# Sparse attention in a graph network: one-hot matrices in a narrow and a wide size, the summing matmuls six tiles behind them, one exponential for two rows, the edge weights applied one row later

## The chip, the cores and the metric

The kernel runs on one core of one Trainium2 chip. The metric is the device time of one execution in microseconds (us). The kernel before took 4278.34 us, the median of three runs (4271.37 to 4294.40).

## What is computed

The reference is a stack of four blocks over 6250 nodes with 256 features each: a graph convolution, a mixture of experts whose routing is a graph attention, a second graph convolution, and a second mixture of experts. The change is in the second block only. Cut to what matters (`_L0_ffn_ref`), it is:

```python
h = (x_flat @ W_gat).reshape(M, HEADS, NUM_EXPERTS)          # 4 heads, 4 experts
src = concat([edge_index[0], loops]); dst = concat([edge_index[1], loops])
e = leaky_relu(a_src[src] + a_dst[dst], 0.2)
ee = exp(e - e_max[dst])
denom = segment_sum(ee, dst)
msg = h[src] * (ee / (denom[dst] + 1e-16))[:, :, None]
agg = segment_sum(msg, dst) + b_gat                          # 131072 edges
scores = layernorm(agg).reshape(M, HEADS, NUM_EXPERTS).mean(1)
topk_s, topk_i = top_k(scores, 2); w = softmax(topk_s)
out = sum over experts of  gate * (gelu(x @ W1[e] + b1[e]) @ W2[e] + b2[e])
```

So each edge needs an attention weight, an exponential of a sum of two node values, and the weighted values of the edges are added up by destination node.

## The kernel before, in words

The program is built by a layer that tracks which instruction reads and writes which buffer, adds the semaphore waits, and gives out buffers from pools of fixed depth (`bufs`). It orders the instructions of each engine by itself: an instruction keeps about the place in which the Python code issues it, unless its buffer is not yet free in the layer's own reckoning; then later instructions go ahead of it. After that each engine runs its instructions strictly in that order.

By the time of the attention stage the edges have been sorted by destination. They stand in tiles of 128 edges, one edge to a partition; `tiles2` lists 84 rows (`NA`) with 8 tiles each (`G`), fewer in the last eleven, 612 tiles in all. The destinations of one tile lie within n neighbouring blocks of 128 nodes, with n from 1 to 7 (`NM` is 7). In most rows the first and the last tile are wide (4 to 7 blocks) and the six between them have at most 3. From row 68 on nearly all tiles are wide, and the last rows have one tile each.

The sum by destination is a matmul. For a tile, VectorE writes a one-hot matrix `E` of 128 edges by n times 128 nodes in bf16 (`spread_out`, L1964): one where the edge's destination is the node. TensorE then multiplies it with the tile's values (`add_up`, L1986), one matmul for each block, and adds the tiles of a row up in the PSUM banks `po`; after the row's last tile VectorE adds `po` to `acc` (L1997). The values come in three bf16 parts, so that the sum is as exact as in fp32: they stand in `pays0` and `pays1`, which the rows use in turn.

One pass of the main loop has number k and works on five rows at once. `fetch(k)` starts the gathers of row k from `gat_dram` into `sg` (GpSimd's indirect DMAs, L1173). `score(k - 2)` multiplies the one-hot rows `rb` with the nodes' values on TensorE (`pa`, L1909). `weigh(k - 3)` picks from `pa` (L1926), sums (L1931), adds the gathered value (L1932), applies the leaky ReLU (L1933) and the exponential on ScalarE (L1934). `weight(k - 3, 0)`, at the end of the same pass, multiplies the gathered values with the exponentials (`pay`, L1946) and writes the first bf16 part (L1951); its steps 1 and 2 (L1953 to L1956) follow in the next pass. `spread_out` runs on row k - 4, two tiles in each of four places of the pass, and `add_up` runs `LAG` tiles behind it:

```python
EB, LAG = 6, 4
Es[g, j] = wk.tile([P, NM, P], BF16, name="E", bufs=EB)
g, j = divmod(there * G + q - LAG, G)        # the tile that add_up takes
```

The pools set how far the engines can run apart: six `E` buffers, all as wide as the widest tile, four `sg`, two `z`, two `pays`.

Between these steps a `slot` is called five times in a pass. It advances three queues of other work. `experts1` computes all experts of the block for all nodes: in each step four fp32 products `ph` (L1160) with Gelu on ScalarE (L1787), or four products `py` (L1160) and their bias on VectorE (`ys`, L1803), written to DRAM. `routing` holds `gates`, the normalisation and the choice of experts for windows whose sums are complete. `steps` holds `node_values`, which adds the chosen experts to `x_all` (L2185) and prepares the next block: a square root (L2196), transposes (L2215, L2226) and the table `hp_dram` (L2229); in the first passes it holds `edge_columns`, which reads the edges of the next block into `hp` and `ht` tiles. In the first 17 passes `count_last` also counts edges of one node (`q`, `b`, L2005 to L2017). The Exp, Gelu and Sqrt functions each need another table in ScalarE, and the program has an ACT_TABLE_LOAD wherever the function changes.

After the loop the queues are emptied, and the next block starts to gather from `hp_dram` (`hg`).

Of the kernel before, what the change touches and what calls it, by code (L numbers as in the profile page):

```python
# [9 lines left out]
F32 = mybir.dt.float32  # L10
# [7 lines left out]
P = 128  # L18
# [889 lines left out]
BF16 = mybir.dt.bfloat16  # L908
# [3 lines left out]
def kernel(ctx: ExitStack, tc: tile.TileContext, a: dict, out: bass.AP):  # L912
# [78 lines left out]
    with ExitStack() as fast:  # L991
# [845 lines left out]
        with (  # L1837
# [35 lines left out]
            pa_both = psa.tile([P, 2, G, 256 // G], F32, name="pa")  # L1873
            assert NM * H <= 256 // G
            HG = G // 2
            EB, LAG = 6, 4
            rows, near, got, pas, zs, pay, Es, pos = {}, {}, {}, {}, {}, {}, {}, {}

            def tiles_of(g, half):
# [7 lines left out]
                return rb  # L1887

            def fetch(g):
                got[g] = wk.tile([P, G, GW], F32, name="sg", bufs=4)  # L1890
                for j in range(len(tiles2[g])):
                    gather(got[g][:, j, :], gat_dram, src2[:, g * G + j : g * G + j + 1])

# [29 lines left out]
            def weigh(g):  # L1923
                m, n = len(tiles2[g]), union[g][2]
                za = wk.tile([P, G, NM, H], F32, name="za", bufs=1)[:, 0:m, 0:n, :]
                V.tensor_mul(  # L1926
                    za, pas.pop(g)[:, 0:m, 0 : n * H].rearrange("p g (b h) -> p g b h", h=H),
                    near.pop(g)[:, 0:m, 0:n].unsqueeze(3).to_broadcast([P, m, n, H]),
                )
                z = wk.tile([P, G, H], F32, name="z")[:, 0:m, :]  # L1930
                V.tensor_reduce(z, za.rearrange("p g b h -> p g h b"), axis=AX.X, op=OP.add)  # L1931
                V.tensor_add(z, z, got[g][:, 0:m, HV:])  # L1932
                V.scalar_tensor_tensor(z, z, 0.2, z, op0=OP.mult, op1=OP.max)  # L1933
                SC.activation(z, z, AF.Exp)  # L1934
                zs[g] = z

            for (u0, u1, _), some in zip(union, tiles2):
                assert {b for lo, n in some for b in range(lo, lo + n)} == set(range(u0, u1))
# [19 lines left out]
            def spread_out(g, j):  # L1958

                if j >= len(tiles2[g]):  # L1960
                    return
                n = tiles2[g][j][1]
                Es[g, j] = wk.tile([P, NM, P], BF16, name="E", bufs=EB)
                V.tensor_scalar(  # L1964
                    Es[g, j][:, 0:n, :].rearrange("p b k -> p (b k)"), nodes16[:, 0 : n * P],
                    bits.bitcast(F32)[:, g * G + j : g * G + j + 1], None, op0=OP.is_equal,
                )
# [272 lines left out]
            def edge_columns():  # L2240

                GP.iota(from_i, pattern=[[P, NC]], base=0, channel_multiplier=1)
                V.tensor_scalar(from_n, from_i, float(NS), None, op0=OP.mult)
                V.tensor_copy(from_i, from_n)
                V.tensor_scalar(from_i, from_i, 8, None, op0=OP.logical_shift_right)
                V.tensor_copy(from_n, from_i)
                V.tensor_scalar(from_n, from_n, -44.0, 0.0, op0=OP.add, op1=OP.max)
                V.tensor_scalar(from_n, from_n, float(NP - NW), None, op0=OP.min)
                for c in range(NC):
                    n = min(P, T1 - c * P)  # L2250
                    at = slice(c * P, c * P + n)
                    for name, none in (("src", 0), ("dst", 2**24), ("edge_weight", 0)):
                        ap = n6.tile([P, P], F32, name="hp")
                        raw = ap.bitcast(I32)
                        ap = ap if name == "edge_weight" else raw
                        full = min(c * P + n, C1) - c * P
                        if full < n:
                            V.memset(raw, none)
                            e = a[name][C1 * P : E1].rearrange("(o p) -> o p", o=1)
                            SY.dma_start(ap[full:n, 0 : E1 - C1 * P], e)  # L2260
                        rows_of = a[name][c * P * P : (c * P + full) * P]
                        SY.dma_start(ap[0:full, :], rows_of.rearrange("(t p) -> t p", p=P))
                        yield False
                        f = n6.tile([P, P], F32, name="ht")
                        if name == "dst":
                            V.tensor_scalar(
                                f[0:n, :], raw[0:n, :], from_n[0:n, c : c + 1], None,
                                op0=OP.subtract,
                            )
                        else:  # L2270
                            V.tensor_copy(f[0:n, :], ap[0:n, :])
                        yield False
                        pt = psy.tile([P, 2, D], F32, name="py")[:, 0, 0:n]
                        TE.transpose(pt, f[0:n, :], ident[0:n, 0:n])
                        if name == "src":
                            g = n6.tile([P, P], F32, name="ht")[:, 0:n]
                            V.tensor_scalar(g, pt, 0.0, float(N), op0=OP.is_lt, op1=OP.mult)
                            V.tensor_add(g, g, pt)
                            V.tensor_scalar(
                                src_of[:, at], g, 0.0, float(N - 1), op0=OP.max, op1=OP.min  # L2280
                            )
                        else:
                            SC.activation((dst_of if name == "dst" else ew)[:, at], pt, AF.Copy)
                        yield False

                hit = wk.tile([P, G, P], BF16, name="rb")
                hit = hit.rearrange("p g k -> p (g k)")[:, 0:T1]
                V.tensor_scalar(hit, dst_of, -0.5, None, op0=OP.is_gt)
                V.scalar_tensor_tensor(
                    hit, dst_of, NW - 0.5, hit, op0=OP.is_lt, op1=OP.mult  # L2290
                )
                V.tensor_reduce(good2[:, 5:6], hit, axis=AX.X, op=OP.add)
# [23 lines left out]
                    steps.append([node_values(ws), False])  # L2316

            def slot(n=1):
                if n and (k < NA or k == NA + 5 or slots[0] % 5 == 0):
                    advance(layers, n)  # L2320
                slots[0] += 1
                run(steps, False)
                load_outputs()
                start_steps()
# [5 lines left out]
            def complete(t1):  # L2330

                while ends and ends[0] <= t1:
                    waiting.append((passed[0], ends[0] - passed[0]))
                    passed[0] = ends.pop(0)
# [6 lines left out]
            ]  # L2341
            remaining = [min(u[0] for u in union[g:]) for g in range(NA)] + [T]
            counted = False
            for k in range(NA + 5):
                if k < NA:
                    fetch(k)
                if k == 1:
                    own_edges()
                now, here, there = k - 2, k - 3, k - 4

                def spread_and_sum(i):

                    for q in (2 * i, 2 * i + 1):
                        if there in range(NA):
                            spread_out(there, q)
                        g, j = divmod(there * G + q - LAG, G)
                        if g in range(NA):
                            add_up(g, j)

                if there in range(NA):  # L2360
                    weight(there, 1)
                spread_and_sum(0)
                slot()
                if now in range(NA):
                    score(now, 0)
                slot()
                if there in range(NA):
                    weight(there, 2)
                spread_and_sum(1)
                if here in range(NA):  # L2370
                    weigh(here)
                tables()
                run(routing, False)
                slot()
                spread_and_sum(2)
                slot()
                if now in range(NA):
                    score(now, 1)
                run(routing, False)
                slot(int(k < 62))  # L2380
                if here in range(NA):
                    weight(here, 0)
                spread_and_sum(3)
                for _ in range(4):
                    if last_columns:
                        count_last(*last_columns.pop(0))
                if not last_columns and not counted:
                    routing.append([last_edges(), False])
                    counted = True
                if counted and k - 5 in range(NA):  # L2390
                    complete(remaining[k - 4])
            V.tensor_reduce(good2[:, 0:1], acc[:, :, 3 * HV], axis=AX.X, op=OP.add)
            k = NA + 5
            while layers or steps or routing or waiting or done["begun"] < T:
                slot()
                tables()
# [400 lines left out]
```

## Time and profile before

| what | value |
| --- | --- |
| median of three runs | 4278.34 us |
| profiled execution | 4285.28 us |
| its span, first to last instruction | 4283.5 us |
| mean granted TensorE clock | 0.831 |
| attention stage in the span | about 1580 to 2920 us |
| TensorE, VectorE, ScalarE, GpSimd busy in the stage | 1020, 704, 576, 597 us of 1340 |
| granted clock in the stage | 0.87 |

The profile is of one execution, 6.9 us above the median. Busy time is the time in which an engine has at least one instruction at work. A row of a group of instructions gives the line, the engine, the operation, the tiles that are written and read, the form, the count, the busy time, the mean duration in ns, and the idle time of the engine just before them with what ended it. A row of the waits gives the engine and the instruction that waited, what ended the wait, the sum in us, how often, and the longest. "issue" means that the profile shows nothing that was waited for, and "remote" that a semaphore ended the wait and no instruction of the record is near enough to be its source.

### The profile page before, as it was taken

To read this page: it belongs to the slowest core of one execution; us is meant where nothing else is said; L and a number is where in the kernel's file an instruction comes from. 1 tells how busy PE (TensorE), PEld (TensorE's weight loads), DVE (VectorE), ACT (ScalarE), POOL (GpSimd) and SP (SyncE) were. 2 spreads that over 40 slices of the span, in tenths; PEclk is the share of its full clock that TensorE was granted. 3 is DMA by queue.
4 is the path that set the end of the run, shared out by engine and by line. 5 is a ranking of instruction groups with operands and counts; after the bars stand their busy time and mean duration, and the time that the engine had idled before them with its cause. 6 is when DMAs were issued, how large, how long until landed. Compare 5 with 4: busy or idle time off the path is not lost.

```text
span 4283.5 us, 59672 instructions
## 1 busy us (share of the span) xinstructions
PE 3272.3 (76%) x19189; PEld 2500.2 (58%) x19189; DVE 2166.2 (51%) x6247; ACT 1188.7 (28%) x2203; POOL 2257.1 (53%) x2720
## 2 busy tenths in 40 slices
PE   6798888888888785777887877785346777877787
PEld 4566666666666564566665666573244555555566
DVE  7576666666555444545463544575123333333344
ACT  4122222222222232334444343463011211211123
POOL 1655655566565544345454444422666666665651
PEclk9899999999999897888998988796567667677678
DMA  5677776777676642223333332343111111111110
GB/s 172 158 172 164 167 161 157 161 171 165 159 168 153 147 108 58 61 65 100 84 99 78 81 89 67 87 109 90 45 46 52 47 51 51 50 51 48 53 47 19
DMA packets 698942, 429.43 MB, mean 100 GB/s; under 512 B 530968, under 2 KB 639563, under 8 KB 698620
## 3 DMA queue, kind: packets, MB, share of 16 engines
q0 software_dynamic: 88512, 177.73, 17.3%
q1 hardware_dynamic: 366812, 188.25, 16.4%
q10 hardware_dynamic: 243296, 59.53, 7.0%
q8 instruction: 155, 2.54, 0.3%
q14 instruction: 167, 1.37, 0.1%
HBM read 382.75 MB, written 42.50 MB: 99 GB/s over the span
## 4 chain that ended last, share of the span: by engine, by line
PE 36%; another core or an unknown queue 14%; issue 6%; DVE 5%; ACT 3%; DMA 1%; POOL 1%; DVEq 0%; ACTq 0%; SPq 0%
PE ph L1160 13%; PE py L1160 11%; PE pe L2662 5%; PE pt L1160 2%; PE po L1986 2%; PE pa L1909 1%; DVE eq L2641 1%; POOL hg L1173 1%; DVE E L1964 1%; DVE x_all L2617 1%; ACT L1787 0%; ACT hh L1787 0%; PE pe L1609 0%; PE pt L1154 0%
## 5 line engine op out<-in xcount | busy, mean ns | idle before, releaser
L1173 POOL DMA_INDIRECT h<-y_dram,src x882 | 858.4, 973 | 669.0 <-issue 485.7
L1173 POOL DMA_INDIRECT hg<-hp_dram,src x831 | 784.9, 944 | 490.7 <-issue 225.0
L1173 POOL DMA_INDIRECT sg<-gat_dram,src x612 | 593.8, 970 | 723.1 <-DVE pay L1946 313.8
L1160 PE MATMUL ph<-w1b,et 128*128 128x256 f32 x3528 | 868.2, 398 | 32.8 <-issue 26.9
L1160 PEld LDWEIGHTS ph<-w1b,et 128*128 128x128 f32 x3528 | 680.3, 198 | 204.4 <-issue 114.3
L1160 PE MATMUL py<-w,hh 128*128 128x256 f32 x1568 | 454.0, 428 | 105.6 <-issue 54.5
L2662 PEld LDWEIGHTS pe<-eq,hg 128*128 128x128 f32 x2036 | 375.3, 261 | 189.8 <-issue 117.5
L2662 PE MATMUL pe<-eq,hg 128*128 128x96 f32 (+15 forms) x2036 | 386.4, 342 | 126.2 <-issue 67.2
L1586 DVE TENSOR_TENSOR h<-ph,h 128x1536 f32<-128x1536 f32 x147 | 258.2, 1757 | 421.1 <-remote 158.6
L1160 PE MATMUL ph<-b_all,w 128*128 128x256 f32 (+1 forms) x1600 | 458.9, 426 | 11.8 <-issue 11.5
L2641 DVE TENSOR_SCALAR eq<-px,dst,ew 128x96 f32<-128x96 f32 x831 | 261.1, 367 | 320.1 <-remote 131.4
L1587 ACT ACTIVATE h<-h 128x1536 f32<-128x1536 f32 x147 | 218.2, 1484 | 728.6 <-DMA ea<-in_edge_attr_dram 288.4
L1160 PEld LDWEIGHTS py<-w,hh 128*128 128x128 f32 x1568 | 308.1, 210 | 171.1 <-issue 70.2
L1160 PEld LDWEIGHTS ph<-b_all,w 128*128 128x128 f32 x1600 | 316.9, 214 | 55.5 <-issue 17.4
L1964 DVE TENSOR_SCALAR E<-nodes,bits 128x256 bf16<-128x256 bf16 (+5 forms) x612 | 187.6, 340 | 194.4 <-remote 73.3
L1609 PE MATMUL pe<-h,eq 128*32 128x257 f32 x3168 | 256.7, 416 | 36.3 <-issue 35.2
L1568 DVE STREAM_TRANSPOSE et<-ea 128x1536 f32<-128x1536 f32 x147 | 260.5, 1773 | 12.7 <-issue 9.3
L1787 ACT ACTIVATE hh<-ph,b 128x256 f32<-128x256 f32 (+1 forms) x400 | 166.5, 467 | 306.8 <-remote 166.5
L1160 PE MATMUL py<-ew,g 65*128 65x256 f32 x392 | 146.6, 503 | 57.5 <-DVE x_all L2617 42.1
L1609 PEld LDWEIGHTS pe<-h,eq 128*32 128x32 f32 x3168 | 104.7, 116 | 143.6 <-issue 91.1
L1986 PE MATMUL po<-pays,E 128*128 128x61 bf16 x2116 | 120.0, 199 | 48.1 <-issue 41.8
L1160 PE MATMUL ph<-b_all,ew 128*128 128x512 f32 (+2 forms) x256 | 115.4, 576 | 53.4 <-ACT g L2577 33.8
(355 smaller groups left out, 3971.7 us busy)
## 6 DMA issues: line engine op xcount, KB each, us to landing
ea<-in_edge_attr_dram ACTq DMA_DIRECT2D x588, 96.0 KB
ea<-in_edge_attr_dram SPq DMA_DIRECT2D x588, 96.0 KB
w<-in_L_ffn_W_dram SPq DMA_DIRECT2D x48, 512.0 KB
y<-ys SPq DMA_DIRECT2D x96, 256.0 KB
rb<-low_dram SPq DMA_DIRECT2D x84, 256.0 KB
h<-y_dram,src POOLq DMA_INDIRECT x882
hg<-hp_dram,src POOLq DMA_INDIRECT x831
gtab<-y SPq DMA_DIRECT2D x100, 128.0 KB
```

The costliest lines, as they stand in the source:

```text
L1160: TE.matmul(dst, lhs(c), rhs(c), start=c == 0, stop=c == n - 1)
L1173: GP.indirect_dma_start(out=dst, out_offset=None, in_=table[0:NP, :], in_offset=IndirectOffsetOnAxis(ap=idx, axis=0),)
L1568: V.transpose(et[q].rearrange("p c m k -> p m c k"), ahead.pop(q).rearrange("p i m (c k) -> p (i m) c k", c=2),)
L1586: V.tensor_add(h, ph.pop(q), h)
L1587: SC.activation(h, h, AF.Relu)
L1609: TE.matmul(sums[w][b * Q : (b + 1) * Q, :], eq[k][:, j, at], h[:, i * NT + j, 0:WS], start=g == 0 and j == NT - 1, stop=g == last_of[b] a ...
L1787: SC.activation(hidden[u][:, f, :n, :], ph[:, f - f0, :n, :], AF.Gelu, bias=b1[:, e, f : f + 1],)
L1909: TE.matmul(pas[g][:, j, 0 : n * H], rows[g][:, j, :], part[:, i, b0 : b0 + n, :].rearrange("p t h -> p (t h)"), start=i == 0, stop=i == 2,)
L1964: V.tensor_scalar(Es[g, j][:, 0:n, :].rearrange("p b k -> p (b k)"), nodes16[:, 0 : n * P], bits.bitcast(F32)[:, g * G + j : g * G + j + 1 ...
L1986: TE.matmul(pos[g][bank][:, to * HP : (to + 1) * HP], E[:, b - b0, :], pays[g % 2][:, j, :], start=bank not in begun, stop=bank not in lat ...
L2641: V.tensor_scalar(equals[k][:, j, :], lanes[:, 0:NW], dst_of[:, t : t + 1], ew[:, t : t + 1], op0=OP.is_equal, op1=OP.mult,)
L2662: TE.matmul(sums[b][:, lo - t0 * P : hi - t0 * P], hg[:, j, :], eq[:, j, lo - n0 : hi - n0], start=False, stop=after >= (t0 + n) * P,)
```

## The change

There are five edits. The one-hot matrices come from two pools: eight buffers of 3 blocks for tiles with n up to 3 (`E`), three buffers of 7 blocks for the others (`Ew`). `LAG` is 6 instead of 4. The exponential is taken at every odd row for that row and the row before, in one instruction where the two have as many tiles and in two instructions one after the other where not; for this `z` holds two rows. `weight` runs one row later (steps 0, 1 and 2 on rows k - 4, k - 5, k - 5), and `spread_out` and `add_up` with it, so that the loop has one pass more and `sg` five buffers. In `edge_columns`, `ht` has one buffer, and the tile for wrapped sources takes the name `hp`.

```diff
-            EB, LAG = 6, 4
+            NARROW, LAG = 3, 6
...
-                got[g] = wk.tile([P, G, GW], F32, name="sg", bufs=4)
+                got[g] = wk.tile([P, G, GW], F32, name="sg", bufs=5)
...
-                z = wk.tile([P, G, H], F32, name="z")[:, 0:m, :]
+                if g % 2 == 0:
+                    zs[g] = wk.tile([P, 2, G, H], F32, name="z")
+                both = zs[g - g % 2]
+                z = both[:, g % 2, 0:m, :]
...
-                SC.activation(z, z, AF.Exp)
-                zs[g] = z
+                if g % 2:
+                    for i in range(2):
+                        zs[g - 1 + i] = both[:, i, 0 : len(tiles2[g - 1 + i]), :]
+                    if len(tiles2[g - 1]) == m:
+                        SC.activation(both[:, :, 0:m, :], both[:, :, 0:m, :], AF.Exp)
+                    else:
+                        for i in range(2):
+                            SC.activation(zs[g - 1 + i], zs[g - 1 + i], AF.Exp)
...
-                Es[g, j] = wk.tile([P, NM, P], BF16, name="E", bufs=EB)
+                if n <= NARROW:
+                    Es[g, j] = wk.tile([P, NARROW, P], BF16, name="E", bufs=8)
+                else:
+                    Es[g, j] = wk.tile([P, NM, P], BF16, name="Ew", bufs=3)
...
-                        f = n6.tile([P, P], F32, name="ht")
+                        f = n6.tile([P, P], F32, name="ht", bufs=1)
...
-                            g = n6.tile([P, P], F32, name="ht")[:, 0:n]
+                            g = n6.tile([P, P], F32, name="hp")[:, 0:n]
...
-                if n and (k < NA or k == NA + 5 or slots[0] % 5 == 0):
+                if n and (k < NA or k == NA + 6 or slots[0] % 5 == 0):
...
-            for k in range(NA + 5):
+            for k in range(NA + 6):
...
-                now, here, there = k - 2, k - 3, k - 4
+                now, here, there = k - 2, k - 3, k - 5
...
-                if here in range(NA):
-                    weight(here, 0)
+                if k - 4 in range(NA):
+                    weight(k - 4, 0)
...
-                if counted and k - 5 in range(NA):
-                    complete(remaining[k - 4])
+                if counted and k - 6 in range(NA):
+                    complete(remaining[k - 5])
```

More of the change, by code (lines that the diff above doesn't have):

```diff
@@ L1933, in weigh @@
                 V.scalar_tensor_tensor(z, z, 0.2, z, op0=OP.mult, op1=OP.max)
-                SC.activation(z, z, AF.Exp)
-                zs[g] = z
+                if g % 2:
[6 more added lines that the diff above has]
+                            SC.activation(zs[g - 1 + i], zs[g - 1 + i], AF.Exp)
+            assert NA % 2 == 0
             for (u0, u1, _), some in zip(union, tiles2):
@@ L2389 @@
                     counted = True
-                if counted and k - 5 in range(NA):
-                    complete(remaining[k - 4])
+                if counted and k - 6 in range(NA):
+                    complete(remaining[k - 5])
             V.tensor_reduce(good2[:, 0:1], acc[:, :, 3 * HV], axis=AX.X, op=OP.add)
-            k = NA + 5
+            k = NA + 6
             while layers or steps or routing or waiting or done["begun"] < T:
```

## The prediction

> **What bounds the kernel now.** I read the stage first. The page puts TensorE at 76% of the whole span with its clock falling to 0.6 to 0.9 in places; the change touches only the attention stage, so its own stretches matter, from the busy time by stage:
>
> ```profile
> core 0: us, PE busy (x) PEld busy (x) DVE busy (x) ACT busy (x) POOL busy (x), PEclk, DMA share, GB/s
> 1580.00:2920.00 1340.00, 1020.24 (x7623) 821.31 (x7622) 703.55 (x2490) 576.38 (x1095) 596.61 (x618) 0.87 0.32 83
> 1640.00:2810.00 1170.00, 899.58 (x6614) 720.24 (x6614) 593.74 (x2024) 478.76 (x894) 541.10 (x558) 0.87 0.31 80
> 2810.00:2920.00 110.00, 96.12 (x856) 81.16 (x855) 86.72 (x364) 85.67 (x173) 21.74 (x22) 0.95 0.45 123
> ```
>
> TensorE leads with 1020 of 1340 us; no other engine is over 53% except in the last 110 us, where rows 69 to 83 run and three engines are near 80%. So what can be won is TensorE's idle time, 320 us, and the clock it loses. Who ends its waits, TensorE's waits in 1580 to 2920:
>
> ```profile
> PE py L1160 <- issue: 56.7, 58, 3.7
> PE po L1986 <- issue: 41.8, 54, 2.5
> PE py L1160 <- ACT hh L1787: 34.8, 17, 4.8
> PE py L2016 <- DVE q L2010: 34.0, 8, 7.0
> PE py L2016 <- DVE ys L1803: 26.6, 1, 26.6
> ```
>
> No row names `E`: the sums do not wait for a one-hot matrix by name. The two L2016 rows are edge counting in the first 17 passes, which stays. What the change can reach is the wait for Gelu and part of "issue". What ScalarE does in the stage, by groups:
>
> ```profile
> line engine op names shapes xcount | busy us, mean ns | idle before us <-releasers
> L1787 ACT ACTIVATE hh<-ph,b 128x256 f32<-128x256 f32 x378 | 158.7, 471 | 302.3 <-remote 166.5 <-PE ph L1160 57.5 <-PE po L1986 44.8
> L1787 ACT ACT_TABLE_LOAD x100 | 128.3, 1283 | 70.5 <-remote 37.9 <-PE ph L1160 10.2 <-PE po L1986 8.9
> L1934 ACT ACT_TABLE_LOAD x80 | 102.6, 1283 | 29.7 <-DVE z L1933 24.5 <-issue 3.8
> ```
>
> Half of ScalarE's work is table loads (216 in the stage, 277 us): each row's exponential brings one, and a second to return to Gelu. Last, the waits of VectorE and then of ScalarE in the same stretch:
>
> ```profile
> DVE E L1964 <- remote: 73.3, 29, 8.0
> DVE za L1926 <- remote: 68.6, 17, 7.0
> DVE E L1964 <- PE po L1986: 44.2, 37, 5.1
> ```
>
> ```profile
> ACT hh L1787 <- remote: 166.5, 26, 29.7
> ACT z L1934 <- DVE z L1933: 59.3, 22, 7.6
> ACT pays L1954 <- DVE pay L1953: 47.6, 43, 11.1
> ACT pays L1951 <- DVE pay L1946: 45.0, 33, 3.7
> ```
>
> VectorE stands at `E` until TensorE has released a buffer, ScalarE then stands behind VectorE at `z` and `pay`, and Gelu is queued behind those.
>
> **What the Trainium skill says.** "ScalarE: Activation LUTs", What ACT_TABLE_LOAD costs: 1283 ns for the load and about 1380 ns of drain. The trace agrees on 1283 ns, but shows the next activation right after the load; I count 1283 alone. "TensorE: Matmul & The Clock Gate", the HAM clock gate: the array falls to half its clock after an idle window of some 3.4 us. The trace fits: 0.87 in the stage, matmuls `py` of 428 ns on average where the shortest take 376. The same page gives ScalarE and VectorE strict order, which is why one wait holds all behind it. "Perfetto Trace Analysis", Tensor Engine Instruction: the recorded end of a matmul is modelled. That fits the "remote" rows: VectorE and ScalarE wait for TensorE after its recorded end. So part of TensorE's idle time is work that the record does not show, and I discount it.
>
> **The change part by part.** The profiled execution took 4285.3 us, 6.9 above the median of 4278.3; the sum is made against it.
>
> (a) Paired exponentials. By the order of the built program the stage has 149 table loads instead of 221: 36 fewer for Exp, 35 for Gelu, one for Sqrt. 72 x 1283 ns = 92.4 us. Of 84 Exp (229 ns) 45 stay; the 39 paired ones grow by some 32 ns each (201 ns for 4 elements, 229 for 32), so 8.9 - 1.2 = 7.7 us. ScalarE loses 100 of 576 us. It is not the bound; what reaches TensorE is a share of its waits for ScalarE. All rows with an ACT releaser in TensorE's list add up to 68 us (34.8 for `hh`, the others under 10 each). Of the "issue" rows ahead of the same instructions (L1160, L2226, L2215: 74 us) I take half: 105 us. A third of the loads goes, and with it a sixth of ScalarE's busy time; its waits at `z` get shorter since only odd rows have one. I take a quarter of 105: -26 us. Bounds 0 (all that idle time is unrecorded work) and -60.
>
> (b) Clock. TensorE's idle time falls by 26 of 320; the same share of the lost 0.13 is 0.011, times 1020: -11 us. Bounds 0 and -30.
>
> (c) Eight narrow buffers, `LAG` 6. The instruction counts on TensorE and VectorE do not change (2116 `po` matmuls, 612 `E`). By the program's order `E` of tile t waited for the sums of tile t - 6 (447 tiles); it now waits for t - 10 (217), t - 12 (84) or t - 15 (31). But the layer places each `E` as soon as its buffer is free, so it still stands close behind the sum that frees it: VectorE's 190 us of waits at `E` largely stay, and what is queued behind them (`ys`, `z`, `pay`) too. TensorE has its matrix ten tiles ahead instead of four, but it did not wait for it by name; a fifth of the 41.8 us of "issue" ahead of `po`: -8 us. Bounds -40 (all of it) and +20 (VectorE held longer at one wait).
>
> (d) Three wide buffers. From tile 544 on nearly all tiles are wide, and `LAG` 6 asks for more matrices than there are: 52 `E` now wait for the sum three tiles before. Queued behind are `ys` (686 ns), `acc` (655) and the next `E` (461); TensorE waits for that next `E`. Between release and need the order leaves TensorE other work (`ph`, `py`, `pa`) of 4 us in the middle, before 8, and under 1.5 us for some ten tiles; there I count 1 us each: +10. Bounds 0 and +40 (52 x 0.76, an `E` and half a `ys`).
>
> (e) Weights one row later. `weight(g, 0)` overwrites the `pays` that row g - 2 used. Before, that row's last sum came two quarters of a pass earlier; with `LAG` 6 it comes one quarter earlier. The order shows 57 such waits on TensorE instead of 32, with 0.9 us of TensorE's work in between instead of 2.8 (median). Behind L1951 on ScalarE stand Gelus, and behind those `py`. The trace had 1.5 us of this wait in all, so the 25 new ones get 0.2 us: +5. Bounds 0 and +40 (57 x 0.7).
>
> (f) One pass more. The last passes have one tile each and took 8.4 to 1.9 us; one more, and two more windows of `node_values` behind the last sum (9 of 49 writes of `hp_dram` instead of 7): +5. Bounds 0 and +15.
>
> (g) At nothing: the fifth `sg`, since `fetch(k)` needs the buffer that `weight` read in pass k - 1, before and after, under GpSimd's 44 waits for `pay` that stay; and `ht` with one buffer, since its 21 transposes lie in the first passes, where TensorE works on experts. Without that cover each would cost one 0.3 us copy, 6 us. SP's order changes by a pass for `rb`, which is loaded a row ahead.
>
> Sum: -26 - 11 - 8 + 10 + 5 + 5 = -25 us: 4260 against the profiled execution, **4253 against the median**. About 0.5% (21 us) is what a measurement of this kernel can tell from no change.
>
> **Rivals.** *The lockstep was the limit.* If VectorE's waits at `E` (73 + 44 + 59 in rows for other matmuls, some 180 us) do go with the deeper ring, half of them, 90 us, returns: about 4185. For it: ScalarE's 150 us behind VectorE. Against: the place of `E` right behind its release.
>
> *Nothing moves.* TensorE's idle time is mostly unrecorded work, and relief of ScalarE lands in more waiting for `ph`: 4275. For it: `hh` waits 166 us "remote" after TensorE's recorded ends.
>
> *Slower: the short rings.* ScalarE is held at L1951 for `pays`, and VectorE at `Ew` from row 68 on. It decides once TensorE runs more than about 1 us behind what the order assumes, as the "remote" waits of up to 8 us suggest it often does. Price: 57 x 0.7 = 40 and 52 x 0.6 = 31, with 26 of gains kept: +45, so 4323.
>
> **How the numbers follow.** The likeliest case (0.46) is the sum, with 4225 to 4275 as its own range; 0.36 of it lies under 4257, 0.10 within 0.5%. The lockstep case 0.16, all faster. Nothing moves 0.16 (0.14 same, 0.02 slower). Short rings 0.22 (0.20 slower, 0.02 same). Faster 0.52, same 0.26, slower 0.22. The range reaches halfway into the outer cases: 4188 to 4320.
>
> **What would show it.** In the profile after: 80 Exp loads become about 44 and 100 Gelu loads about 65, ScalarE near 476 us in the stage; the wait of `py` for `hh` under 30 us; the clock near 0.88. `E` still waits for TensorE between rows 5 and 67. Wrong if L1951 waits over 20 us for `po`, if the stretch of rows 69 to 83 grows by more than 15 us, or if VectorE's waits at `E` drop below 60 us.

## The result, and the profile after

The changed kernel takes 4404.14 us (median of 4 runs, 4391.17 to 4411.05) against 4286.37 us for the kernel before in the same comparison (the three runs above and a fourth): ratio 1.027, 95% interval 1.023 to 1.032. The prediction said 4253 us, with a range of 4188 to 4320; the kernel is slower. The profiled execution took 4401.36 us, 116 us more than the 4285.28 us of before.

Busy time by stage after the change, in the columns of the stage view shown of before (length, then busy time of TensorE, weight loads, VectorE, ScalarE, GpSimd, granted clock, DMA share, GB/s). The three stretches answer to 1580 to 2920, 1640 to 2810 and 2810 to 2920:

```profile
1580.00:3045.00 1465.00, 1024.20 (x7604) 824.95 (x7602) 699.50 (x2485) 474.62 (x976) 590.36 (x613) 0.81 0.28 76
1640.00:2925.00 1285.00, 906.70 (x6587) 727.18 (x6587) 589.79 (x2033) 391.22 (x796) 529.15 (x551) 0.81 0.27 73
2925.00:3045.00 120.00, 102.75 (x930) 86.05 (x928) 94.37 (x387) 76.72 (x168) 22.78 (x22) 0.92 0.43 120
```

The whole loss lies here: 1340 us became 1465. No engine has more to do. TensorE and VectorE are within 5 us of before, and ScalarE has 102 us less, as the change intends. The 125 us are idle time on every engine, 115 of them in the middle rows and 10 in the last; 103 lie between the first and the last `po` matmul. ScalarE's groups in the stage:

```profile
L1787 ACT ACTIVATE hh<-ph,b 128x256 f32<-128x256 f32 (+1 forms) x392 | 163.2, 466 | 589.2 <-remote 325.6 <-PE ph L1160 155.0 <-PE po L2000 88.2
L1787 ACT ACT_TABLE_LOAD x65 | 83.4, 1283 | 21.6 <-PE ph L1160 11.0 <-PE py L2030 4.6 <-PE po L2000 4.0
L1941 ACT ACT_TABLE_LOAD x38 | 48.8, 1283 | 0.7
...
L1944 ACT ACT_TABLE_LOAD x6 | 7.7, 1283 | 0.1
```

The loads went as counted: 80 for Exp and 100 for Gelu before are 44 and 65 after (L1941 is the exponential of two rows, L1944 that of one). But Gelu now stands idle for 589 us where it stood for 307 (all its forms), and the largest part, "remote", is time after TensorE's recorded end. The waits of the stage show the same on three engines (waiting tile, line and releaser, then total, times, longest):

```profile
PE py L1160 <- issue: 80.3, 55, 10.9
PE py L1160 <- ACT hh L1787: 49.2, 11, 10.8
...
DVE za L1926 <- remote: 122.4, 12, 16.3
DVE ys L1803 <- remote: 78.7, 7, 35.0
...
POOL sg L1173 <- DVE pay L1957: 504.8, 34, 30.8
```

Of before, the `za` row was 68.6 us in 17 waits of at most 7.0. TensorE's waits for Gelu have become fewer and longer: 49.2 us for `hh` in 11 waits, where it was 34.8 in 17. The last row is the one that leads to the cause. The prediction knew its counterpart (the 44 waits for `pay` of its step (g)) and set it aside. GpSimd's waits for `pay`, which releases the `sg` buffers that it gathers into, in the attention stage of the kernel before:

```profile
POOL sg L1173 <- DVE pay L1946: 313.8, 44, 12.5
```

Ten waits fewer, and each on average twice as long: GpSimd now waits for two rows at a time. What follows such a wait, from the timeline of after (start, duration, engine, line, operation, tiles; in brackets idle time before it and its releaser):

```profile
2292.72 0.32 DVE L1957 TENSOR_TENSOR pay<-sg,z 128x160 f32<-128x160 f32 x1
2293.30 0.94 POOL L1173 DMA_INDIRECT sg<-gat_dram,src  x1 [17.72 <-DVE ag L2135]
2294.55 0.96 POOL L1173 DMA_INDIRECT sg<-gat_dram,src  x1 [0.30 <-issue]
...
2296.55 0.45 PE L1909 MATMUL pa<-part,rb 128*128 128x24 bf16 x12
...
2297.19 0.32 DVE L1957 TENSOR_TENSOR pay<-sg,z 128x160 f32<-128x160 f32 x1
...
2298.81 1.97 PE L1160 MATMUL ph<-b_all,w 128*128 128x256 f32 x8
...
2303.32 0.19 PE L2000 MATMUL po<-pays,Ew 128*128 128x61 bf16 x1 [1.18 <-issue]
...
2303.38 0.39 DVE L1926 TENSOR_TENSOR za<-pa,A 128x224 f32<-128x224 f32 x1 [5.80 <-remote]
...
2305.49 0.47 PE L1160 MATMUL py<-w,hh 128*128 128x256 f32 x1 [0.35 <-issue]
...
2312.13 0.94 POOL L1173 DMA_INDIRECT sg<-gat_dram,src  x1 [0.30 <-issue]
2315.38 0.69 DVE L1803 TENSOR_TENSOR ys<-py,b 128x512 f32<-128x512 f32 x1 [10.01 <-remote]
...
2316.24 0.84 ACT L1787 ACTIVATE hh<-ph,b 128x256 f32<-128x256 f32 x2 [15.01 <-remote]
2316.76 2.08 PE L1160 MATMUL py<-w,hh 128*128 128x256 f32 x4 [10.81 <-ACT hh L1787]
```

The profile puts the wait of the first gather down to `ag`, which ended 0.2 us after `pay`; what the gather needs is the buffer that `pay` has read. The two `pay` multiplications of a pair of rows stand 4.5 us apart. Each frees one `sg`, so GpSimd issues two rows' gathers, 16 in a row, one every 1.25 us from 2293.3 to 2313.1. About 3 us into this run TensorE's results stop arriving: `pa` is recorded as done at 2297.0, but `za`, which needs only it on TensorE, starts at 2303.38; `ph` is recorded as done at 2300.8, but Gelu gets it at 2316.24. TensorE itself first issues haltingly (1.18 us before one `po`) and then stands 10.8 us, because its next `py` needs that Gelu. The first result comes through 2.3 us after the last gather's end.

I call a stretch held when it runs for over 2 us from the recorded end of a TensorE instruction that raises a semaphore to the next time that this semaphore is raised. Between the first and the last `po` matmul there are 74 such stretches before (273 us together) and 68 after (297 us), and in both kernels every one begins within a run of gathers, give or take 2 us, and ends at most 3.1 us after the run (the runs cover 56% of that time before and 51% after). So the hold is nothing new. In a run of 8, as before, it begins 5 us into the run and ends with it (medians of 67), some 4 us in which the work in flight can bridge much; in a run of 16 one stretch reaches 11.8 us, which it can't. Stretches of over 6 us: 7 before, with 49 us together, and 18 after, with 137. Between the same two `po` matmuls TensorE's idle time went from 272 to 385 us, and its gaps of over 3.5 us from 19 with 87 us together to 30 with 226; the clock fell as well, from 0.87 to 0.81 in the stage.

A rival reading is that the gathered values now come too late. The trace is against it: after the change the addition of the gathered value (`z`, L1935) waited 0.2 us in the whole stage, and the multiplication at L1957 0.5 us.

### The profile page after: what moved, and what is told of

Its sections match the earlier page's. It is cut to its first block, busy times and chain, and to the rows that moved or that the text cites. A ratio compares the mean times of both kernels' runs of the same rounds, so it can differ in the third digit from the quotient of the medians.

```text
span 4399.6 us, 59574 instructions
## 1 busy us (share of the span) xinstructions
PE 3276.1 (74%) x19189; PEld 2503.6 (57%) x19189; DVE 2158.9 (49%) x6247; ACT 1088.9 (25%) x2092; POOL 2249.5 (51%) x2720
## 3 DMA queue, kind: packets, MB, share of 16 engines
q1 hardware_dynamic: 366812, 188.25, 15.9%
## 4 chain that ended last, share of the span: by engine, by line
PE 36%; another core or an unknown queue 14%; issue 8%; DVE 5%; ACT 2%; POOL 2%; DMA 1%; ACTq 0%; DVEq 0%; SPq 0%; POOLq 0%
PE ph L1160 14%; PE py L1160 11%; PE pe L2676 5%; PE pt L1160 2%; POOL hg L1173 2%; PE po L2000 2%; PE pa L1909 1%; DVE eq L2655 1%; DVE x_all L2631 1%; PE pe L1609 1%; PE pt L1154 0%; DVE x_all L2199 0%; DMA rb<-low_dram 0%; PE pe L2671 0%
## 5 line engine op out<-in xcount | busy, mean ns | idle before, releaser
L1173 POOL DMA_INDIRECT sg<-gat_dram,src x612 | 588.8, 962 | 854.1 <-DVE pay L1957 504.8
L1978 DVE TENSOR_SCALAR E<-nodes,bits 128x256 bf16<-128x256 bf16 (+2 forms) x422 | 113.6, 300 | 155.3 <-remote 78.2
L1160 PEld LDWEIGHTS py<-ew,g 65*128 65x128 f32 x392 | 90.9, 245 | 90.5 <-issue 42.7
```

What stands on the lines that cost most here:

```text
L1160: TE.matmul(dst, lhs(c), rhs(c), start=c == 0, stop=c == n - 1)
L1173: GP.indirect_dma_start(out=dst, out_offset=None, in_=table[0:NP, :], in_offset=IndirectOffsetOnAxis(ap=idx, axis=0),)
L1978: V.tensor_scalar(Es[g, j][:, 0:n, :].rearrange("p b k -> p (b k)"), nodes16[:, 0 : n * P], bits.bitcast(F32)[:, g * G + j : g * G + j + 1 ...
```

## The experiments

My theory, called **bursts** in the expectations: the exponential of two rows lets both rows' multiplications run back to back, so the gathers come in runs of 16 (I wrote 18 there, having counted one more semaphore event in each row), and TensorE's results are held too long to be bridged. Its rivals: **rings** (three wide buffers, `LAG` 6 and two `pays`) and **ScalarE order** (where the paired exponential and its loads stand). The experiments ran on different chips, so each is read against the kernel before on its own chip.

**One exponential per row in the changed kernel.**

```diff
-                if g % 2 == 0:
-                    zs[g] = wk.tile([P, 2, G, H], F32, name="z")
-                both = zs[g - g % 2]
-                z = both[:, g % 2, 0:m, :]
+                z = wk.tile([P, G, H], F32, name="z")[:, 0:m, :]
...
-                if g % 2:
...
+                SC.activation(z, z, AF.Exp)
+                zs[g] = z
```

> The changed kernel with one exponential per row; rings, LAG 6 and the later weights stay. Theory 'bursts' (the paired exponential brings the two multiplications that release `sg` 3 to 7 us apart, so GpSimd issues two rows' gathers, 18 in a row, and TensorE's completions are held up for as long as such a run lasts): releases are one row apart again, runs of 9, the time comes back to 4260 to 4300, the table loads to about 220, the clock of the stage to 0.86 or more. Theory 'rings' (three wide buffers, LAG 6 and two `pays` cost the time): stays at 4380 to 4420. Theory 'ScalarE order' (the exponential of two rows and its loads stand ahead of Gelu at a bad place): 4260 to 4300 too.

4210.78 us against 4219.73: ratio 0.9975 (0.9955 to 0.9995). The loss is gone, with the rings and the later weights still there, so together these cost nothing.

**The paired exponential with the old ring.** The changed kernel with the one-hot matrices of before:

```diff
-            NARROW, LAG = 3, 6
+            EB, LAG = 6, 4
...
-                if n <= NARROW:
-                    Es[g, j] = wk.tile([P, NARROW, P], BF16, name="E", bufs=8)
-                else:
-                    Es[g, j] = wk.tile([P, NM, P], BF16, name="Ew", bufs=3)
+                Es[g, j] = wk.tile([P, NM, P], BF16, name="E", bufs=EB)
```

> The kernel before with the paired exponential, the weights one row later and the fifth sg buffer, but with its own ring of six wide one-hot matrices and LAG 4. Bursts: 4370 to 4430, runs of 18 gathers. Rings: 4240 to 4290, about the kernel before or a little faster. ScalarE order: 4370 to 4430.

4364.83 us: 1.032 (1.024 to 1.040). The rings are not the cause. ScalarE order is still possible; the next two runs are against it.

**The changed kernel with the odd row's buffer held back.**

```diff
-                        got.pop(g)[:, 0:m, 0:HV].rearrange("p g (x h) -> p g x h", h=H),
+                        got[g][:, 0:m, 0:HV].rearrange("p g (x h) -> p g x h", h=H),
...
                     V.tensor_sub(pay[g], pay[g], parts[0])
+                    if g % 2:
+                        V.tensor_add(
+                            wk.tile([P, 1], F32, name="held", bufs=1),
+                            got[g][:, 0, 0:1], pay[g][:, 0, 0:1],
+                        )
+                    got.pop(g)
```

> The changed kernel, whole, with one tiny addition in every odd row that reads that row's `sg` after the first rest is taken from `pay`, so that its buffer is released some 20 us later, about midway to the next row's; 42 more VectorE instructions of about 0.15 us. Bursts: runs of 9 gathers, 4240 to 4300, with the table loads still 149. Rings: 4380 to 4420. ScalarE order: 4380 to 4420.

4218.1 us: 0.999 (0.997 to 1.002). One addition on a 128 x 1 tile in every second row takes the whole loss away; exponentials, loads (44 and 65) and rings are those of the changed kernel. Its stage, in the columns of the stage view:

```profile
1600.00:2857.00 1257.00, 985.55 (x7510) 795.44 (x7509) 687.15 (x2454) 469.39 (x960) 558.88 (x575) 0.88 0.34 86
```

ScalarE's relief is there (469 us busy) and the clock is back at 0.88.

**The kernel before with its gathers paired.** A fifth `sg` and one small addition in every second row serve the pairing; nothing else differs.

```diff
-                got[g] = wk.tile([P, G, GW], F32, name="sg", bufs=4)
+                got[g] = wk.tile([P, G, GW], F32, name="sg", bufs=5)
...
+                    if g % 2:
+                        V.tensor_add(
+                            wk.tile([P, 1], F32, name="held", bufs=1),
+                            got.pop(g - 1)[:, 0, 0:1], pay[g][:, 0, 0:1],
+                        )
+                        got.pop(g)
                     SC.activation(parts[0], pay[g], AF.Copy)
```

> The kernel before (one exponential per row, LAG 4, six wide buffers, weights as before) with a fifth sg buffer and the release of every even row's sg put off, by one tiny addition, until the odd row's multiplication: nothing but the pairing of the gathers. Bursts: runs of 18 gathers, 4370 to 4430, clock of the stage near 0.81. Rings and ScalarE order: 4280 to 4300.

4376.68 us: 1.036 (1.029 to 1.043). Its stage, in the same columns:

```profile
1600.00:3049.00 1449.00, 1022.85 (x7511) 813.86 (x7510) 688.63 (x2459) 567.39 (x1072) 569.01 (x594) 0.81 0.29 75
```

ScalarE's busy time is that of before, the idle time and the clock are those of after. The pairing of the gathers alone makes the loss, so ScalarE order falls too. The six kernels side by side (the chips of the first two are not known, the other four ran on one chip); the second column is TensorE's work between one release of an `sg` buffer and the next, added up along the order of the built program (0.43 us for a 128x256 fp32 matmul, which stands in the trace as two records 0.22 us apart, and 0.03 for a bf16 one):

| Kernel | Work between releases, us | Runs of 8 / of 16 gathers | First to last `po`, us | Clock in it | Ratio |
|---|---|---|---|---|---|
| before | mostly 8 to 15 | 63 / 3 | 1249 | 0.88 | 1 |
| after | 2 to 6, then 16 to 25 | 12 / 28 | 1351 | 0.82 | 1.027 |
| one exponential per row | mostly 8 to 14 | 60 / 4 | 1190 | 0.89 | 0.998 |
| paired, old ring | 2 to 6, then 16 to 26 | 8 / 30 | 1353 | 0.82 | 1.032 |
| after, odd row held back | mostly 7 to 15 | 55 / 6 | 1194 | 0.89 | 0.999 |
| before, gathers paired | 0 to 2, then 18 to 28 | 0 / 34 | 1384 | 0.82 | 1.036 |

That the pairing makes the loss is shown in both directions. That it does so through held results is read from the traces, and not from their sum: with the odd row held back 289 us are held, nearly as much as the 297 after, and nothing is lost. What goes with the loss is how long one hold lasts. The three kernels with runs of 8 have 4 to 7 stretches of over 6 us, with 28 to 49 us together, and TensorE is idle for 238 to 272 us between the first and the last `po`; the three with runs of 16 have 16 to 18, with 133 to 157 us, and 368 to 385 us idle.

**Parts of the change without the bursts.** The second experiment's kernel with the odd row held back, and the kernel before with the two sizes and `LAG` 6 alone:

> The kernel before with the paired exponential, weights one row later and the fifth sg buffer, with its own rings and LAG 4, and with the odd row's `sg` held back by the tiny addition: the paired exponential without the pairing of the gathers. If ScalarE's relief (72 table loads fewer, 100 us) reaches TensorE as the prediction had it (26 us and 11 of clock): ratio 0.989 to 0.994 to the kernel before. If TensorE's idle time comes from the runs of gathers alone: 0.997 to 1.003.

> The kernel before with the two sizes of one-hot matrices and LAG 6 only; exponentials, weights and sg as before. By the prediction's steps (c) and (d), -8 and +10 us: ratio 0.998 to 1.002. If the ring of ten is worth something once the gathers come singly (as in the run with one exponential per row, 0.9975): 0.995 to 0.998. If three wide buffers cost: above 1.003, in the rows from 69 on.

These two runs and the next two fell on another kind of chip: the kernel before took 3355.53 us, and in their profiles only 1 to 3 stretches are held in the whole stage. The stage of the run with the rings alone:

```profile
1340.00:2219.00 879.00, 850.54 (x7458) 721.79 (x7457) 672.52 (x2380) 552.35 (x1057) 591.19 (x593) 0.99 0.48 122
```

TensorE is busy for 97% of it. The paired exponential without bursts, with the later weights and the extra pass, gave 0.9988 (0.9979 to 0.9998), 4 us; the rings alone 1.0007 (0.9994 to 1.0019), nothing.

**Gathers in two runs of four, and half of the gathers.** Both start from the kernel before; the second leaves out half of the gathered values and sets them to zero:

```diff
...
+                elif marks and len(tiles2[g]) > HG:
+                    n = len(tiles2[g]) - HG
+                    GP.tensor_copy(
+                        got[g][:, HG : HG + n, 0:1],
+                        marks[-1].unsqueeze(2).to_broadcast([P, n, 1]),
+                    )
+                for j in range(half * HG, min(half * HG + HG, len(tiles2[g]))):
...
+                        V.tensor_copy(marks[-1], Es[there, 1][:, 0, 0:1])
+                    fetch(k, 1)
```

```diff
-                for j in range(len(tiles2[g])):
+                for j in range(min(HG, len(tiles2[g]))):
                     gather(got[g][:, j, :], gat_dram, src2[:, g * G + j : g * G + j + 1])
+                if len(tiles2[g]) > HG:
+                    GP.memset(got[g][:, HG:, :], 0.0)
```

> The kernel before with each row's eight gathers in two runs of four: between them GpSimd waits for an element that VectorE copies from the one-hot matrix of the row's second tile, half a row later (one tiny copy on VectorE and one on GpSimd in a row). If TensorE is held up in proportion to the length of a run beyond what the work in flight bridges: runs of 4, the held stretches over 2 us fall from about 270 us to under 150, ratio 0.975 to 0.990. If the price is per gather and not per run: 0.997 to 1.005, the held time unchanged. If neither, and the gathers come too late instead: above 1.005.

> The kernel before with only the first four gathers of each row; the other four tiles of sg are set to zero by one GpSimd instruction, so half of the gathered data is left out. It measures what a gather costs TensorE. If it is the issuing of gathers that holds TensorE: held stretches over 2 us fall to half or less, ratio 0.970 to 0.985. If the gathers only happen to lie beside stretches in which TensorE is behind anyway: held time and ratio stay, 0.997 to 1.003.

On the chip that holds nothing: 1.0004 (0.9991 to 1.0016) and 0.993 (0.991 to 0.995). Neither says anything of holds.

**The changed kernel again, half of the gathers again, and fills in place of the other half**, on a chip where the kernel before took 4274.9 us. The fills:

```diff
                     GP.memset(got[g][:, HG:, :], 0.0)
+                    for _ in range(12):
+                        GP.memset(wk.tile([P, 256], F32, name="busy", bufs=1), 0.0)
```

> The changed kernel once more, on whichever chip this call gets. Two calls have shown two kinds of chip: in one (kernel before near 4220) TensorE's completions are held during GpSimd's runs of gathers, in the other (near 3355) they are not. Bursts: on a chip of the first kind the ratio is 1.025 to 1.035 again; on one of the second kind nothing is held and the ratio is 0.995 to 1.005, although the gathers come in pairs of rows there too. Rings or ScalarE order: 1.02 or more on either kind.

> The kernel before with only four gathers in a row (half of the gathered data left out). On a chip that holds TensorE during gathers: held stretches over 2 us fall to half or less of the 270 us of the kernel before, ratio 0.970 to 0.985. On one that does not: 0.993 as measured.

> The same with four gathers in a row, and GpSimd kept busy with twelve fills of a scratch tile (128 x 256) in place of the other four. On a chip that holds TensorE: if it is the issuing of gathers that holds it, like the run with half of the gathers alone, within 0.5%; if any work of GpSimd does, near the kernel before, 0.995 to 1.005. On the other kind of chip: like the run with half of the gathers.

The changed kernel: 1.029 (1.025 to 1.033), as before. Half of the gathers: 3903.65 us, 0.915 (0.911 to 0.918), far below what I expected; 58 us are held instead of 273, and the stage is

```profile
1600.00:2542.00 942.00, 872.67 (x7487) 731.36 (x7487) 676.87 (x2402) 563.07 (x1068) 312.05 (x371) 0.98 0.40 111
```

With the fills GpSimd is as busy as before (593 us), and the ratio is 0.931 (0.927 to 0.936): the fills cost about 2%, but the gathers are most of it. I had expected one or the other; it is both, unevenly. The stretch from the first to the last `po` was 859 us where nothing is held; it is 916 with half of the gathers, in runs of four, about 1190 to 1249 with a row's gathers in a run and 1351 to 1384 with two rows'. From one row to two the number of gathers is the same and only the run grows; the 916 has fewer gathers too, so it does not separate the two.

**All gathers in two runs of four, on a chip that holds**, alone, with the paired exponential (odd row held back), and in the changed kernel (odd row held back); the second run of four waits for the one-hot matrix of the second, fourth and sixth tile. The kernel before took 4275.34 us.

> The kernel before with each row's gathers in two runs of four, half a row apart, once more, since the first such run fell on a chip that holds nothing. On a chip that holds TensorE during gathers: if the first four of a run are nearly free, as the run with half of the gathers suggests (0.915), all the data is gathered and the ratio is still 0.92 to 0.95, the stretch of the sums under 1000 us; if the price is per gather, 0.995 to 1.005. On the other kind of chip 1.000 again.

> The kernel before with the paired exponential, weights one row later, the odd row's sg held back, and each row's gathers in two runs of four (the second waits for the one-hot matrix of the fourth tile). If ScalarE's relief counts once the holds are gone: 0.5 to 1% faster than with four and four alone (0.91 to 0.945); if not: equal to it within 0.3%.

> The changed kernel, whole, with the odd row's sg held back and each row's gathers in two runs of four (the second waits for the one-hot matrix of the sixth tile). A version that may beat both: 0.91 to 0.945 of the kernel before on a chip that holds TensorE during gathers; rings of ten tiles are worth 0 to 0.5% beside the same with six wide buffers.

Alone 4165.46 us, 0.975 (0.970 to 0.980); with the paired exponential 0.981 (0.976 to 0.986); in the changed kernel 0.983 (0.978 to 0.989). The first is faster than both kernels, but gives only a part of what I expected (0.92 to 0.95, the stretch of the sums under 1000 us; it is 1141): in 42 of 71 rows GpSimd did not have to wait for the element, and mostly the eight still ran as one. Nor are runs of four free: of the 69 held stretches of the first of these kernels, 21 with 68 us together begin in them. The other two have ScalarE's relief in addition and gain nothing by it; their second run of four waits for a different tile, so their difference from the first is not explained.

**The changed kernel a third time**, to meet a chip that holds nothing:

> The changed kernel once more, to meet a chip of the kind that holds nothing (one call in four did). There, bursts of two rows' gathers should cost nothing: 0.995 to 1.005. On a chip that holds TensorE: 1.025 to 1.035 as twice before, and nothing new.

1.027 (1.022 to 1.031): this chip, too, was one that holds. What a burst costs where nothing is held stays open.

## Why the prediction was wrong

**The step that failed is (g)**: "the fifth `sg`, since `fetch(k)` needs the buffer that `weight` read in pass k - 1, before and after, under GpSimd's 44 waits for `pay` that stay". It put this term at nothing, since it counted in passes. But the odd row's multiplication, once the exponential is shared, has the same exponential to wait for as the even row's, and the built order puts it close behind. The 44 waits did not stay: 34, and 504.8 us for 313.8. The order of the built program showed this ahead of any run (2 to 6 us of work between two releases, then 16 to 25); I read it for the table loads and for `E`, and not for what the moved multiplication releases. With (g), step (e) priced the later weights only by the buffer that they overwrite, `pays`, and not by the buffer that they free.

**A reading failed as well.** I took the "remote" waits for work of TensorE that the record does not show, and discounted its idle time for it. With half of the gathers TensorE's busy time in the stage falls to 873 us and it has 69 us idle instead of 320: most of those waits were held results. None of the three signs of being wrong that the prediction named came, though the kernel is slower: L1951 (L1962 after) waited 5.7 us for `po` by name, the last rows grew by 10 us, and the waits at `E` stayed at 120. None of them looks at GpSimd. The signs of being right came for ScalarE alone (475 us), and not for the wait of `py` for `hh` (49 us, forecast under 30) or the clock (0.81, forecast 0.88).

**(a) The table loads.** The count held: 44 and 65 in the stage, ScalarE 474.6 us busy where 476 was forecast. The term that was mis-sized is the quarter of 105 us that I let reach TensorE: -26. Measured: -4 us on the chip that holds nothing, with (e) and (f) in it, so that the term alone may be somewhat larger; on one that holds, none can be seen (0.999 with the paired exponential, 0.998 without).

**(b) The clock.** In these runs it was lower the longer TensorE was idle between the first and the last `po`: 0.99 with 28 us (the rings alone), 0.98 with 66 (half of the gathers), 0.88 with 272 (before), 0.82 with 385 (after). But the idle time grew, by 113 us: -11 became part of the loss.

**(c), (d) The rings.** VectorE's waits at `E` stay, as said: `E` for "remote" and `po` is 120 us (118 before), and the new `Ew` adds 96. The term -8 was 0: the rings alone give 1.0007, on the chip that holds nothing. The last rows took 10 us more, as (d) had it; what part of that is the rings was not separated.

**(e), (f).** ScalarE waits at L1962 for 5.7 us by the name of `po`, and 27.2 us "remote" in four waits of up to 15.9; that is as long as Gelu's held wait in the timeline (15.01). The extra pass was not measured by itself.

**The rivals.** *Short rings* had the right side (4323), by luck, for the wrong reason: with the old ring the kernel is as slow, and with the short rings and one exponential per row nothing is lost. *Nothing moves* describes the change without the bursts best: 0.999 in the whole. *The lockstep* fell: with the ring of ten nothing came back.

## What to carry to other kernels

When one instruction is made to serve two rows, list what each instruction behind it frees, and on which queue: here the cost came through GpSimd, which the change does not touch, since two buffers came free together. The spacing of releases can be read from the built order, before any run. And a long "remote" wait is not to be put down to unrecorded work until it has been laid beside what the other engines issue in that moment.

## What the runs showed of the hardware

On four of the five chips that the experiments met (the kernel before at 4220 to 4285 us), TensorE's semaphores were raised late while GpSimd issued indirect gathers: in runs of 8 from about the fifth gather to the end (medians of 67 stretches of the kernel before), in runs of four from about 3 us on (21 stretches with half of the gathers). Other stages of the program were longer there too. On the remaining one (3355 us) GpSimd issued its gathers at the same pace, about 1.25 us each, in runs of over a hundred, and TensorE was held for under 11 us in the stage. The Trainium skill, "SBUF — State Buffer", SBUF: two separate sides, says that TensorE never waits on another engine for its ports; no run here shows whether a port, the semaphores or something else is what waits. Each chip was met once. Why they differ, and what holds the results, stays open.
